# A two-layer graph attention kernel: x1 stored in the place of the head values, and two row tiles of layer 1 held back into the next entry

## The chip, the cores and the metric

The kernel runs on one core of one Trainium2 chip. The time is device microseconds from one execution of the whole program; the figure for a kernel is the median over several executions. A profile is one further look at one execution: it names engines PE (TensorE matmul; PEld is its weight load), DVE (VectorE), ACT (ScalarE), POOL (GpSimd) and SP (the engine whose queue issues the DMAs here). A "unit" below is one step of layer 0, a "row tile" 128 rows.

## The reference

Input `x` has 8 batch entries of 2048 nodes with 256 features; `adj` is one 2048 x 2048 matrix of edges for all entries.

```python
# layer 0: 8 heads of 32 features
x_proj = einsum('bnd,hdf->bhnf', x, W)
e = leaky_relu(e_src[..., :, None] + e_dst[..., None, :], 0.2)
e = e + (softplus(beta_tilde) * log(adj + 1e-6))[:, None]
attn = softmax(where(adj > 0, e, -big))
h = einsum('bhij,bhjf->bhif', attn, x_proj)          # heads side by side: 256 features
x1 = layernorm(x + h @ W_out.T)
# layer 1: one head
e = leaky_relu((x1 @ W1) @ (x1 @ W2).T, 0.2)
attn = softmax(where(adj > 0, e, -1e12))
out = layernorm(x1 + relu(attn @ (x1 @ W3)))
```

Everything is float32.

## The kernel before

Each batch entry passes through layer 0 (class `Gat`) and then layer 1 (class `Dot`). While layer 1 of entry b-1 runs, layer 0 of entry b runs between its pieces; the first entry's layer 0 runs alone, with the projections of all other entries, and the last entry's layer 1 runs alone.

**Layer 0** has 64 units per entry: four pairs of heads (`hp`) by 16 column tiles (`jt`). In a unit (`step`, L288) SP loads one row of the edge matrix (`mt`, 1 MB, two buffers), VectorE makes one 128 x 2048 tile `s` for each of the two heads (L304, four buffers), and TensorE multiplies them into `val` (the weighted sum of values, L313) and, except in the units of `SUMMED` (1, 3, 6, 8, 11, 13), into `den` (the softmax denominators, L319). The `s` of those six units are added up instead: the first by ACT (L317), the others by VectorE one unit later (L311), and one last product with ones brings the sum into `den`. After unit 15 of a pair, `finish` (L333) has ACT copy `val` to `ht` and `den` to `dn`; SP brings the denominators to a `rc` tile (L346), VectorE inverts them (L347), SP stores them to `rec_d` (L348). After each second pair SP reads them back spread over partitions, `rb` (L354), and VectorE multiplies `ht` by `rb` (L356). `ht` is two tiles, one for each two pairs, of 128 x 2048.

**`output`** (L358) goes over 16 row tiles: two products of `ht` with `wot` to `y` (L369), add of `x` (L371), layer norm (L190: statistics on VectorE, five small ACT instructions), store of x1 to `x1_d` (L373). `x` is first loaded into `h3`, a 128 x 16 x 256 tile in one buffer, by four DMAs (L365); x1 is written there too. **`turn`** (L376) transposes x1 into `x1t` (L384, L385) and replaces x1 in `h3` by x1 times W3 (L389, L391), one row tile behind.

**Layer 1** (`Dot.step`, L429) handles one row tile: transposes of its attention values `p` four at a time (L439, copied by ACT to `pts`, L441), the scores of the next row tile (L413: products `e`, leaky ReLU on ACT, mask and minimum on VectorE at L425, exponential on ACT at L426), 16 products with `h3` into `acc` (L455), and a tail with division, residual, layer norm and store. Every fourth step also makes queries `h1` (L404). `step` calls a function `fill(k)` in three places (start, after the scores, after `acc`), and the main loop puts layer 0 units there.

**Order.** TensorE's instructions stay in the order in which the code writes them (L85). Those of the other engines and of SP's queue are ordered by the framework's scheduler when the program is built; each engine then runs its own list in that order. Tiles of one tag share a ring of buffers: `ht` in the pool `chunk` has three slots of 4 KB per partition, for `dn`, `h1` and others; `mm` is a ring of three PSUM banks for `y`, transposes and scores; `whole` tiles have one buffer each, so a new tile waits until all readers of the last are done.

**Between two entries** (L491 to L507) the loop does: load of `v` for the new entry, layer 1's step 15 of the entry before, two units, `output` with a unit after rows 8 and 16, `turn` with a unit after each second row (8), the first scores, then step 0 with four units and steps 1 to 14 with 48. Layer 0 units only exist while there is a next entry (`fresh`).

Of the kernel before, what the change touches and what calls it, by code (L numbers as in the profile page):

```python
# [9 lines left out]
F32 = mybir.dt.float32  # L10
# [8 lines left out]
P = 128  # L19
# [8 lines left out]
def kernel(  # L28
# [26 lines left out]
    nc = tc.nc  # L55
    B, N, D = x.shape
    H, _, DH = w_proj.shape
    NT = N // P
    KC = D // P
    BK = 512  # L60
    NB = N // BK
    HALF = N // 2
    HP = 2
    NP = H // HP
    IG = BK // P
# [4 lines left out]
    whole = ctx.enter_context(tc.tile_pool(name="whole", bufs=1))  # L70
    wide = ctx.enter_context(tc.tile_pool(name="wide", bufs=2))
    chunk = ctx.enter_context(tc.tile_pool(name="chunk", bufs=2))
# [4 lines left out]
    def mm_tile(name):  # L77
        return ps.tile([P, BK], F32, tag="mm", name=name)

    def wide_tile(name, tag, bufs, dtype=F32):  # L80
        return wide.tile([P, N], dtype, tag=tag, name=name, bufs=bufs)
# [6 lines left out]
    ident = const.tile([P, P], F32)  # L88
# [45 lines left out]
    wot = const.tile([P, KC, D], F32)  # L134
# [8 lines left out]
    for dc in range(KC):  # L143
        t = mm_tile("w12p")
# [45 lines left out]
    def layer_norm(z):  # L190

        st = small.tile([P, nc.vector.BN_STATS_DIM], F32, name="st", bufs=2)
        nc.vector.bn_stats(st, z)
        mv = small.tile([P, nc.vector.BN_AGGR_DIM], F32, name="mv", bufs=3)
        nc.vector.bn_aggr(mv, st)  # L195
        f = small.tile([P, 4], F32, name="f", bufs=3)
        nc.scalar.activation(f[:, 0:1], mv[:, 1:2], AF.Ln, bias=eps_ln)  # L197
        nc.scalar.activation(f[:, 1:2], f[:, 0:1], AF.Exp, scale=-0.5)
        nc.scalar.mul(f[:, 2:3], mv[:, 0:1], -1.0)
        nc.scalar.activation(f[:, 3:4], f[:, 1:2], AF.Identity, scale=f[:, 2:3])  # L200
        nc.scalar.activation(z, z, AF.Identity, bias=f[:, 3:4], scale=f[:, 1:2])  # L201
# [5 lines left out]
    class Gat:  # L207


        def __init__(self, b):  # L210
            self.b = b
            self.units = ((hp, jt) for hp in range(NP) for jt in range(NT))
            self.hts = []
            self.mts = []

        def project(self):
# [10 lines left out]
            def turn(g):  # L227
# [10 lines left out]
                xts.append(xt)  # L238

            turn(0)  # L240
            for g in range(NB):
                if g + 1 < NB:
                    turn(g + 1)
                for k in range(IG):
                    it = g * IG + k
                    t = mm_tile("proj")
                    for kc in range(KC):
                        nc.tensor.matmul(t[:, 0:D + 2 * H], xts[g][:, kc, ts(k, P)], wp[:, kc, :],  # L248
                                         start=(kc == 0), stop=(kc == KC - 1))
                    nc.scalar.copy(v[:, it, :], t[:, 0:D])  # L250
                    nc.scalar.copy(ed[:, it, :], t[:, D:D + H])
                    nc.scalar.copy(es[:, :, it], t[:, D + H:D + 2 * H])
                yield
# [22 lines left out]
        def load(self):  # L276
            self.v = whole.tile([P, NT, D], F32, name="v")
            nc.sync.dma_start(self.v, v_d[self.b])
            self.re = small.tile([P, 2, NT, H], F32, name="re", bufs=2)
            nc.sync.dma_start(self.re, re_d[self.b])  # L280
# [52 lines left out]
        def finish(self, hp):  # L333


            b, lo = self.b, hp % 2 * HP * DH
            if lo == 0:
                self.hts.append(whole.tile([P, N], F32, name=f"ht{hp // 2}"))
            ht = self.hts[-1]
            for s in range(2):  # L340
                nc.scalar.copy(ht[lo:lo + HP * DH, ts(s, HALF)], self.val[ts(s, HP * DH), :])
            dn = chunk.tile([P, HALF], F32, tag="ht", name="dn", bufs=3)
            nc.scalar.copy(dn, self.den)
            rc = small.tile([P, HALF // DH], F32, name="rc", bufs=1)
            for q in range(4):
                nc.sync.dma_start(rc[ts(q, DH), :], dn[q * DH:q * DH + 1, :])  # L346
            nc.vector.reciprocal(rc, rc)  # L347
            nc.sync.dma_start(rec_d[b, hp].rearrange("q (p c) -> (q p) c", c=HALF // DH), rc)  # L348
            if lo == 0:
                return  # L350
            rb = wide_tile("rb", "d", 2)
            for a in range(2 * HP):
                src = rec_d[b, hp - 1 + a // HP, a % HP::HP, :]
                nc.sync.dma_start(rb[ts(a, DH), :].rearrange("p (s i) -> p s i", s=2),  # L354
                                  bass.AP(tensor=src.tensor, offset=src.offset, ap=[[0, DH]] + list(src.ap)))
            nc.vector.tensor_mul(ht, ht, rb)  # L356

        def output(self):  # L358


            b = self.b
            self.h3 = h3 = whole.tile([P, NT, D], F32, tag="h3", name="h3")
            xb = x[b].rearrange("(t p) d -> p t d", p=P)
            for g in range(NB):
                nc.sync.dma_start(h3[:, ts(g, IG), :], xb[:, ts(g, IG), :])  # L365
            for it in range(NT):
                y = mm_tile("y")
                for g, ht in enumerate(self.hts):
                    nc.tensor.matmul(y[:, 0:D], ht[:, ts(it, P)], wot[:, g, :], start=(g == 0), stop=(g == 1))  # L369
                z = h3[:, it, :]  # L370
                nc.vector.tensor_add(z, y[:, 0:D], z)  # L371
                layer_norm(z)
                nc.sync.dma_start(x1_d[b, ts(it, P), :], z)  # L373
                yield

        def turn(self):  # L376

            self.x1t = x1t = whole.tile([P, KC, N], F32, tag="x1t", name="x1t")
            h3 = self.h3
            for it in range(NT + 1):  # L380
                if it < NT:
                    t = mm_tile("tr1")
                    for kc in range(KC):
                        nc.tensor.transpose(t[:, ts(kc, P)], h3[:, it, ts(kc, P)], ident)  # L384
                    nc.scalar.copy(x1t[:, :, ts(it, P)], t[:, 0:D].rearrange("p (k i) -> p k i", k=KC))  # L385
                if it > 0:
                    t = mm_tile("h3p")
                    for kc in range(KC):
                        nc.tensor.matmul(t[:, 0:D], x1t[:, kc, ts(it - 1, P)], w3s[:, kc, :],  # L389
                                         start=(kc == 0), stop=(kc == KC - 1))  # L390
                    nc.scalar.copy(h3[:, it - 1, :], t[:, 0:D])  # L391
                    yield
# [90 lines left out]
    dot = None  # L483
    for b in range(1, B + 1):
        gat, fresh = gats[b - 1], gats[b] if b < B else None

        def layer_0(count):
            if fresh:
                fresh.step(count)

        if fresh:  # L491
            fresh.load()
        if dot is not None:
            dot.step()
        layer_0(2)
        for k, _ in enumerate(gat.output()):
            if k % 8 == 7:
                layer_0(1)
        for k, _ in enumerate(gat.turn()):
            if k % 2 == 1:  # L500
                layer_0(1)
        dot = Dot(gat)
        dot.step(lambda k: layer_0((2, 1, 1)[k]))
        for i in range(NT - 2):
            dot.step(lambda k: layer_0((0, 2 - (i % 2 == 1), 2 - (i % 14 == 13))[k]))
    dot.step()


# [29 lines left out]
```

## Time and profile before

| | |
|---|---|
| median of 7 executions | 4482.95 us (4480.63 to 4486.83) |
| profiled execution, its own time | 4481.61 us |
| its span, first to last instruction | 4479.8 us |
| mean granted TensorE clock | 0.983 |
| `s` on VectorE (L304) | 1024 instructions, 2345 ns each |
| sums on VectorE (L311) | 280 instructions, 2346 ns each |
| first `y` of entries 1 to 8, us from the span's start | 576.9, 1088.5, 1600.2, 2112.1, 2624.1, 3136.0, 3648.0, 4154.6 |

The middle entries are alike, some 512 us apart. In the profile's lines a group reads: start, length, engine, line, operation, tile written <- tiles read, shapes, count; in brackets the idle time of the engine before it and what ended it. Lengths of groups overlap a little, since matmuls are pipelined; the distance between the starts of two neighbours is the better measure. A line of a wait reads: who waited <- for whom, total us, times, longest us. "Granted clock" is the share of TensorE's clock that it was given.

### The profile page before, as it was taken

Reading aid. Unit: us, or ns where it says so; the run is one execution under the profiler, and the core shown is the slowest. Engines: PE = TensorE matmul, PEld = TensorE weight load, DVE = VectorE, ACT = ScalarE, POOL = GpSimd, SP = SyncE. Lnnn points to the kernel's source line nnn. Section 1 sums busy time; section 2 is a strip of 40 time slices with the busy share of each in tenths; the row PEclk is TensorE's granted clock in tenths of the full one; section 3 lists DMA queues with packets and bytes.
Section 4 is the critical chain, followed back from the end, with each engine's and each line's share of the span. In section 5 each row is a group of like instructions: output and inputs, shape, how many; then the busy total and the mean of one; then the engine's idle time right before and its main releaser. Section 6 shows DMA issues by size and latency. Waiting matters only on the chain.

```text
span 4479.8 us, 60564 instructions
## 1 busy us (share of the span) xinstructions
PE 4270.1 (95%) x24924; PEld 2222.4 (50%) x24924; DVE 3649.5 (81%) x2597; ACT 1769.9 (40%) x3739; POOL 4.5 (0%) x14
## 2 busy tenths in 40 slices
PE   6898889999999999999999999999999999999899
PEld 4443335545445544555455554555454554555566
DVE  5788798988989888888998888888988889898222
ACT  5621233334333344333433343333433343333555
POOL 0000000000000000000000000000000000000000
PEclk9999999999999999999999999999999999999999
DMA  7788865556555465555545564555545565554211
GB/s 216 255 302 322 322 211 177 190 187 214 185 184 187 167 220 174 192 187 206 197 172 183 180 220 177 192 192 192 196 173 192 180 220 185 181 181 140 69 50 40
DMA packets 252773, 852.00 MB, mean 190 GB/s; under 512 B 33616, under 2 KB 152400, under 8 KB 174928
## 3 DMA queue, kind: packets, MB, share of 16 engines
q1 hardware_dynamic: 252496, 848.13, 54.5%
q8 instruction: 195, 3.19, 0.3%
q14 instruction: 82, 0.67, 0.0%
HBM read 772.15 MB, written 75.37 MB: 189 GB/s over the span
## 4 chain that ended last, share of the span: by engine, by line
PE 66%; DVE 15%; issue 8%; ACT 4%; DMA 2%; SPq 0%; DVEq 0%; POOL 0%; POOLq 0%
PE acc L455 17%; PE e L420 15%; PE val L329 13%; DVE s L304 10%; PE den L329 9%; PE pt L439 4%; DVE d L311 3%; PE h1p L409 2%; PE proj L248 1%; DMA mt<-mt_d 1%; PE y L369 1%; ACT p L426 1%; PE h3p L389 1%; ACT h L201 1%; DVE p L425 1%
## 5 line engine op out<-in xcount | busy, mean ns | idle before, releaser
L304 DVE SCALAR_TENSOR_TENSOR s<-c,re,mt 128x2048 f32<-128x2048 f32 x1024 | 2351.1, 2345 | 194.9 <-PE den L329 122.2
L329 PE MATMUL val<-s,v 128*32 128x512 f32 x8192 | 1050.3, 605 | 91.1 <-DVE s L304 81.1
L455 PE MATMUL acc<-h,pts 128*128 128x256 f32 x4096 | 950.6, 380 | 14.4 <-ACT pts L441 13.8
L420 PE MATMUL e<-x1t,h 128*128 128x512 f32 x2048 | 903.8, 594 | 0.0
L455 PEld LDWEIGHTS acc<-h,pts 128*128 128x128 f32 x4096 | 748.2, 190 | 107.1 <-ACT pts L441 21.3
L329 PE MATMUL den<-s,re 128*32 128x512 f32 x5504 | 698.8, 596 | 0.0
L311 DVE SCALAR_TENSOR_TENSOR d<-s,re,d 128x2048 f32<-128x2048 f32 x280 | 651.5, 2346 | 0.0
L420 PEld LDWEIGHTS e<-x1t,h 128*128 128x128 f32 x2048 | 379.5, 190 | 449.9 <-issue 417.5
L329 PEld LDWEIGHTS val<-s,v 128*32 128x32 f32 x8192 | 242.7, 110 | 717.5 <-issue 522.0
L441 ACT COPY pts<-pt 128x512 f32<-128x512 f32 x512 | 296.4, 583 | 664.2 <-PE pt L439 663.9
L422 ACT ACTIVATE p<-e 128x512 f32<-128x512 f32 x512 | 303.0, 595 | 430.3 <-PE e L420 430.3
L425 DVE CUSTOM_DVE_ANT_0 p<-p,pen 128x2048 f32<-128x2048 f32 x128 | 293.0, 2289 | 202.8 <-ACT p L422 202.7
L329 PEld LDWEIGHTS den<-s,re 128*32 128x32 f32 x5504 | 192.7, 111 | 416.5 <-issue 414.7
L426 ACT ACTIVATE p<-p,neg 128x2048 f32<-128x2048 f32 x128 | 256.7, 2005 | 274.1 <-DVE neg L425 274.1
L439 PEld LDWEIGHTS pt<-ident,p 128*128 128x128 f32 x2048 | 238.0, 141 | 223.2 <-issue 166.4
L439 PE MATMUL pt<-ident,p 128*128 128x128 f32 x2048 | 318.7, 279 | 5.1 <-ACT p L426 5.1
L463 DVE TENSOR_TENSOR z<-z,x1r 128x256 f32<-128x256 f32 x128 | 54.2, 423 | 199.2 <-ACT z L462 191.1
L462 ACT ACTIVATE z<-acc,rec 128x256 f32<-128x256 f32 x128 | 60.9, 476 | 358.3 <-PE acc L455 333.5
L369 PE MATMUL y<-wot,ht 128*128 128x256 f32 x512 | 135.8, 428 | 37.7 <-DVE ht L356 36.6
L197 ACT ACTIVATE f<-mv,eps_ln 128x1 f32<-128x1 f32 x256 | 74.3, 290 | 203.4 <-DVE mv L195 202.3
L389 PE MATMUL h3p<-w3s,x1t 128*128 128x256 f32 x512 | 133.3, 386 | 12.4 <-ACT x1t L385 12.4
L369 PEld LDWEIGHTS y<-wot,ht 128*128 128x128 f32 x512 | 109.2, 217 | 70.3 <-DVE ht L356 39.4
(81 smaller groups left out, 2110.5 us busy)
## 6 DMA issues: line engine op xcount, KB each, us to landing
mt<-mt_d SPq DMA_DIRECT2D x496, 1024.0 KB, 4.9
c<-c_d SPq DMA_DIRECT2D x64, 1024.0 KB, 6.8
pen<-pen_d SPq DMA_DIRECT2D x128, 512.0 KB, 3.4
xr<-in_x_dram SPq DMA_DIRECT2D x16, 1024.0 KB, 8.2
adj_t<-in_adj_dram SPq DMA_DIRECT2D x16, 1024.0 KB, 6.8
mt_d<-mt SPq DMA_DIRECT2D x16, 1024.0 KB, 5.3
adj_r<-in_adj_dram SPq DMA_DIRECT2D x16, 1024.0 KB, 8.1
rb<-rec_d SPq DMA_DIRECT2D x64, 256.0 KB, 4.8
```

The lines of the kernel that those rows point to most:

```text
L304: nc.vector.scalar_tensor_tensor(sa, self.cs[a], self.re[:, 0, jt, h:h + 1], mt, ALU.max, ALU.mult)
L311: nc.vector.scalar_tensor_tensor(d, sa, e[:, jt - 1, h:h + 1], d, ALU.mult, ALU.add)
L329: nc.tensor.matmul(dst[ts(q, DH), ts(c, BK)], weights[q % 2], s[q % 2][:, ds(q // 2 * HALF + c * BK, BK)], start=start, stop=stop)
L369: nc.tensor.matmul(y[:, 0:D], ht[:, ts(it, P)], wot[:, g, :], start=(g == 0), stop=(g == 1))
L389: nc.tensor.matmul(t[:, 0:D], x1t[:, kc, ts(it - 1, P)], w3s[:, kc, :], start=(kc == 0), stop=(kc == KC - 1))
L420: nc.tensor.matmul(t, self.h1[:, kc, ts(it % IG, P)], self.x1t[:, kc, ts(c, BK)], start=(kc == 0), stop=(kc == KC - 1))
L422: nc.scalar.activation(p[:, ts(c, BK)], t, AF.Prelu, alpha=ALPHA)
L425: nc.vector.tensor_tensor_reduce(p, p, pen, -1.0, FMAX, ALU.add, ALU.min, neg)
L426: nc.scalar.activation(p, p, AF.Exp, bias=neg, scale=-1.0, accum_out=den)
L439: nc.tensor.transpose(t[:, ts(k, P)], p[:, ts(g * IG + k, P)], ident)
L441: nc.scalar.copy(pt, t)
L455: nc.tensor.matmul(acc, now[:, ts(k, P)], self.h3[:, j, :], start=(j == 0), stop=(j == NT - 1))
```

## The change

The two `ht` tiles become one tile of 128 x 16 x 2 x 128 (row tile, half of the features, row in the tile), with one buffer. `output` loads `x` into tiles of the `ht` ring in `chunk`, four row tiles to a load: three at the start, the fourth before row 4. x1 of a row tile is written over the head values of that row tile. `h3` is only claimed in `turn`, and `turn` transposes x1 from the heads' tile.

The main loop leaves steps 14 and 15 of layer 1 until the next entry's turn. Step 14 runs right after the load of `v`, with two units at its end; step 15 runs with 5 rows of `output` at its start, 5 rows and a unit after its first transposes, 6 rows and a unit after its products. The 48 units after `turn`'s first step are spread over 13 steps of layer 1, in the pattern 4, 4, 3. For entry 1, which has no layer 1 before it, the order is the old one. At the end of the program two steps remain instead of one.

```diff
         def finish(self, hp):
...
-            if lo == 0:
-                self.hts.append(whole.tile([P, N], F32, name=f"ht{hp // 2}"))
-            ht = self.hts[-1]
+            if hp == 0:
+                self.ht = whole.tile([P, NT, KC, P], F32, tag="heads", name="ht")
+            ht = self.ht[:, :, hp // 2, :]
             for s in range(2):
-                nc.scalar.copy(ht[lo:lo + HP * DH, ts(s, HALF)], self.val[ts(s, HP * DH), :])
+                nc.scalar.copy(ht[lo:lo + HP * DH, ts(s, NT // 2), :],
+                               self.val[ts(s, HP * DH), :].rearrange("p (t i) -> p t i", i=P))
...
-            nc.vector.tensor_mul(ht, ht, rb)
+            nc.vector.tensor_mul(ht, ht, rb.rearrange("p (t i) -> p t i", i=P))

         def output(self):
             b = self.b
-            self.h3 = h3 = whole.tile([P, NT, D], F32, tag="h3", name="h3")
             xb = x[b].rearrange("(t p) d -> p t d", p=P)
-            for g in range(NB):
-                nc.sync.dma_start(h3[:, ts(g, IG), :], xb[:, ts(g, IG), :])
+            xs = []
+
+            def load(g):
+                xs.append(chunk.tile([P, IG, D], F32, tag="ht", name="xg", bufs=3))
+                nc.sync.dma_start(xs[g], xb[:, ts(g, IG), :])
+
+            for g in range(NB - 1):
+                load(g)
             for it in range(NT):
+                if it == IG:
+                    load(NB - 1)
                 y = mm_tile("y")
-                for g, ht in enumerate(self.hts):
-                    nc.tensor.matmul(y[:, 0:D], ht[:, ts(it, P)], wot[:, g, :], start=(g == 0), stop=(g == 1))
-                z = h3[:, it, :]
-                nc.vector.tensor_add(z, y[:, 0:D], z)
+                for g in range(KC):
+                    nc.tensor.matmul(y[:, 0:D], self.ht[:, it, g, :], wot[:, g, :], start=(g == 0), stop=(g == KC - 1))
+                z = self.ht[:, it].rearrange("p g i -> p (g i)")
+                nc.vector.tensor_add(z, y[:, 0:D], xs[it // IG][:, it % IG, :])
                 layer_norm(z)
...
         def turn(self):
             self.x1t = x1t = whole.tile([P, KC, N], F32, tag="x1t", name="x1t")
-            h3 = self.h3
+            self.h3 = h3 = whole.tile([P, NT, D], F32, tag="h3", name="h3")
...
-                        nc.tensor.transpose(t[:, ts(kc, P)], h3[:, it, ts(kc, P)], ident)
+                        nc.tensor.transpose(t[:, ts(kc, P)], self.ht[:, it, kc, :], ident)
...
         if fresh:
             fresh.load()
-        if dot is not None:
-            dot.step()
-        layer_0(2)
-        for k, _ in enumerate(gat.output()):
-            if k % 8 == 7:
-                layer_0(1)
+        rows = gat.output()
+
+        def output(count):
+            for _ in range(count):
+                next(rows)
+
+        if dot is None:
+            layer_0(2)
+            for k in range(NT):
+                output(1)
+                if k % 8 == 7:
+                    layer_0(1)
+        else:
+            dot.step(lambda k: layer_0((0, 0, 2)[k]))
+            dot.step(lambda k: (output((5, 5, 6)[k]), layer_0((0, 1, 1)[k])))
...
         dot.step(lambda k: layer_0((2, 1, 1)[k]))
-        for i in range(NT - 2):
-            dot.step(lambda k: layer_0((0, 2 - (i % 2 == 1), 2 - (i % 14 == 13))[k]))
+        for i in range(NT - 3):
+            dot.step(lambda k: layer_0((0, 2 - (i % 3 == 2), 2)[k]))
+    dot.step()
     dot.step()
```

More of the change, by code (lines that the diff above doesn't have):

```diff
@@ L212, in __init__ @@
             self.units = ((hp, jt) for hp in range(NP) for jt in range(NT))
-            self.hts = []
             self.mts = []
```

## The prediction

> **What bounds the kernel now.** I read the page's first two parts, then TensorE's waits, then the stretch between two batch entries in order of time, then the busy time of each engine in pieces of that stretch.
>
> ```profile
> span 4479.8 us, 60564 instructions
> PE 4270.1 (95%) x24924; PEld 2222.4 (50%) x24924; DVE 3649.5 (81%) x2597; ACT 1769.9 (40%) x3739; POOL 4.5 (0%) x14
> PE   6898889999999999999999999999999999999899
> DVE  5788798988989888888998888888988889898222
> ```
>
> TensorE is the bound almost everywhere; VectorE (DVE) is second. What can be won without removing matmuls is TensorE's lost time only. Its waits say where that is:
>
> ```profile
> PE val L329 <- DVE s L304: 81.1, 58, 10.9
> PE y L369 <- DVE ht L356: 36.6, 7, 9.1
> PE acc L455 <- ACT pts L441: 13.8, 22, 0.8
> PE h3p L389 <- ACT x1t L385: 12.4, 14, 4.9
> ```
>
> Columns: total us, times, longest. The second line is once per entry at the first product of `output` (seven times: 9.13 in the last entry, so 4.58 in each of the other six). The order of time around one of them, TensorE alone:
>
> ```profile
> 1079.61 3.62 PE L455 MATMUL acc<-h,pts 128*128 128x256 f32 x16
> 1083.16 1.92 PE L329 MATMUL val<-s,v 128*32 128x512 f32 x16
> 1084.90 1.90 PE L329 MATMUL den<-s,re 128*32 128x512 f32 x16
> 1086.62 1.90 PE L329 MATMUL val<-s,v 128*32 128x512 f32 x16
> 1088.45 0.70 PE L369 MATMUL y<-wot,ht 128*128 128x256 f32 x2
> 1093.72 9.51 PE L369 MATMUL y<-wot,ht 128*128 128x256 f32 x30 [4.58 <-DVE ht L356]
> 1103.17 1.92 PE L329 MATMUL val<-s,v 128*32 128x512 f32 x16
> ```
>
> The last row tile of layer 1 ends, two units of layer 0 follow, then `y` stands for the normalised heads. The 30 products after the stall take 9.45 us to the next start; later 32 take 7.10 us. The window view gives the reason, and what comes next (columns: length, then busy time of PE, PEld, DVE, ACT, POOL, then the granted clock, DMA share, GB/s):
>
> ```profile
> 1073.40:1083.20 9.80, 9.18 (x56) 7.68 (x54) 3.44 (x3) 5.01 (x7) 0.00 (x0) 1.00 0.66 222
> 1083.20:1088.50 5.30, 5.30 (x50) 1.47 (x49) 2.68 (x4) 1.90 (x6) 0.00 (x0) 1.00 0.48 121
> 1088.50:1093.70 5.20, 0.65 (x5) 0.24 (x2) 5.17 (x3) 0.00 (x0) 0.00 (x0) 0.89 1.04 327
> 1093.70:1103.20 9.50, 9.47 (x34) 7.62 (x35) 6.30 (x20) 7.58 (x23) 0.00 (x0) 0.70 0.51 189
> 1103.20:1115.70 12.50, 12.50 (x82) 7.32 (x81) 12.35 (x27) 9.89 (x44) 0.00 (x0) 1.00 0.83 274
> 1115.70:1167.40 51.70, 46.98 (x308) 21.23 (x304) 51.70 (x29) 15.26 (x49) 0.00 (x0) 1.00 0.49 167
> 1167.40:1585.10 417.70, 416.31 (x2436) 209.69 (x2432) 370.19 (x237) 158.91 (x271) 0.00 (x0) 1.00 0.53 189
> ```
>
> Three things. After the stall the clock is granted at 0.70, so the stall costs 4.58 plus about 2.8 us (9.45 less 30/32 of 7.10). During step 15 of layer 1 (first row) VectorE works 3.44 of 9.80 us. In `turn` (sixth row) it works all 51.70 us: VectorE, not TensorE, sets the length there. In the last row, fifteen steps of layer 1 with 52 units of layer 0, TensorE loses only 1.4 us and VectorE is at 89%.
>
> **The change part by part.** Counts of matmuls, VectorE, ScalarE (ACT) and DMA instructions stay as they are. What moves is where they stand.
>
> *Prices.* An `s` or a denominator sum on VectorE in a dense run: 2.26 us (four `s` in 9.05). A row's add, statistics and aggregate: 0.43 + 0.43 + 0.18 = 1.03. A `val` or `den` group on TensorE: 1.74 (1083.16 to 1084.90). A step of layer 1 with no layer 0 in it, from the last entry: 4352.28 to 4367.81, 15.53. A row of `output`: 7.10 / 8 = 0.89.
>
> *Steps 14 and 15 held back.* Before, the chain from the last unit to the normalised heads (denominator out, four DMAs to `rc`, reciprocal, `rec_d`, four DMAs to `rb`, multiply) is covered by step 15 and two units, 1073.46 to 1088.4, and is 4.58 short; 4.62 of that is two `s` that VectorE took at 1086.85, ahead of the multiply. After, step 14 (15.53) and two units cover it, and the `s` of those units fit into the step before the multiply is due. I take the `y` stall as gone, and the slow clock with it. What is late next is VectorE. From the end of unit 0 to the end of `turn` it must make `s` for units 2 to 11 (20) and the sums of units 3, 6, 8 (6): 26 x 2.26 = 58.8; 16 rows, 16.5; the tails of steps 14 and 15, 2.1. Together 77.4. So from the start of step 14 to the end of `turn`: 15.53 + 3.46 (unit 0) + 77.4 + 1.85 (last `val`) = 98.2. Before, the same work took 15.53 + 93.95 (1073.46 to 1167.41) = 109.5. At most 11.3 us are saved per transition, if VectorE never rests; its rest before, in the rows, was 3.2 waiting for `y`. I take 4.0 of rest: 7.3 saved, six times, 43.8.
>
> *The last transition* has no layer 0. Before: 9.13, and the 62 products after it 15.41 against 62 x 0.222 = 13.8: some 1.6 more. There the heads were ready 19.3 us after step 15 began, but two `rb` loads were issued at 4155.30, behind an `x` load at 4154.82 that stood for step 15's last reads of `h3`. Without that wait they could go at about 4151.5, so ready after 15.5, against 15.53 of cover. Saved: between 6.9 (all of the 3.8 stays) and 10.7; I take 9.
>
> *x1 in the place of the heads.* `x` goes to three slots of the "ht" ring instead of `h3`; the four loads per entry keep their 512 KB. They wait for `dn` and the last `h1`; the latter is free after step 14's scores, its four acc groups and two units (8.2 + 5.2 us) before the first row, and a load lands in 3.9 to 8.2 us: hidden; without that cover, up to 8.2 once. The fourth load waits for row 3's add. Behind it on SP's queue stand stores of x1 and the next `mt` load, for a unit two dozen us later; `mt` lands in 4.9: hidden, else 4.9. `h3` is now claimed in `turn`; ACT's copies into it wait for step 15's last `acc`, six rows (5.3) and a `val` earlier: hidden. Next entry's first `finish` (SP's four `rc` loads and ACT's copies) waits for `turn`'s transposes, a dot step earlier: hidden. Strided heads: the multiply (2.28) and the copies (1.01) move the same elements; the nearest row for a broken-up operand is the copy to `x1t`, 0.37 for 256 elements as for the plain copy to `h3`, so I take 0.
>
> *Interleaved rows.* Rows in groups of 5, 5, 6 between pieces of step 15. The copies of `pt` (ACT, L441) now share ACT with 16 normalisations (0.29 + 0.19 + 0.20 + 0.29 + 0.60 = 1.57 each). Before shows no such mix; nearest is `turn`'s first copy to `x1t` behind the last norms: 0.80 + 0.24 per transition, and 4.91 in the last. I take the small end, within the 4.0 above; the other end is 4.9 per transition, with slow clock 7.7.
>
> The Trainium skill ("TensorE: Matmul & The Clock Gate", section "Architectural detail") has ScalarE and VectorE as strict first-in first-out queues, while TensorE may pull only weight loads ahead. This speaks against the change: a `pt` copy queued behind norms that wait for VectorE can't pass them. By the rule at its hardest the ten norms before it would hold it to the far end of the last paragraph; by the row, about 1 us.
>
> *Layer 0 packed tighter.* 48 units over 13 steps, not 14. By the last window, steps 0 to 13 would have 416.3 - 15.5 = 400.8 on TensorE and 370.2 - 2.3 - 1.0 = 366.9 on VectorE: 92%. On average there is room; locally not always. Units 11 to 14 in one step: VectorE 4 x 4.52 + 2 sums x 4.52 + 2.26 + 1.03 = 30.4, TensorE 15.53 + 6 x 1.74 = 26.0; units 4 to 7: 30.4 against 27.7. Four `s` buffers let VectorE be about one unit (4.5) ahead, which absorbs most. I take 1.5 lost per entry, seven entries, 10.5; ends 0 and 8 (4.4 + 2.7 and a little).
>
> **Sum.** 43.8 + 9 - 10.5 = 42.3. The profiled execution took 4481.6 (span 4479.8), 1.3 under the median: 4481.6 - 42.3 + 1.3 = 4440.6, so 4441.
>
> **The rivals.**
> *A, VectorE becomes the bound in the dot steps.* For it: 92%, two steps per entry over 100%, and the largest wait of TensorE is already for `s`. Against it: 89% before lost only 1.4 us in 417.7. It decides from (43.8 + 9) / 7 = 7.5 lost per entry; at 10 the sum is +17, 4500. Slower.
> *B, the wait only moves.* VectorE rests while TensorE does step 15's acc between the row groups, about as long as it rested before; then the transition gains 2 (part of the slow clock) and 12 + 6 - 10.5 = 7.5 comes out: 4475, within 0.2%. For it: `turn` stays VectorE's. Against: `s` for the next unit can start as soon as a unit two back is done.
> *C, ACT's queue or the `y` tiles' three PSUM slots stall step 15.* 4.5 of the 7.3 is lost: 6 x 2.8 + 7 - 10.5 = 13, 4470. For it: 4.91 in the last entry; against: 0.80 in the others.
>
> **How the numbers follow.** Forecast 0.58, A 0.16, B 0.09, C 0.17. About 0.2% (9 us) is what a measurement of this kernel can tell from no change: faster 0.58 + 0.17 = 0.75, same 0.09, slower 0.16. The forecast's own range is 4404 (11.3 six times, 10.7 and no loss: 78.5) to 4465. The range given reaches over C and B into A: 4404 to 4486.
>
> **What would show it.** Right: TensorE's wait of `y` for `ht` near zero; clock 1.00 through the rows; the stretch from step 14 to `turn`'s end near 102 us against 109.5; VectorE without rest from step 15 to `turn`'s end; entries about 506 apart instead of 511.9. Wrong: waits of `val` for `s` between the steps of layer 1 (A), VectorE idle for TensorE's `y` or `acc` (B), waits of `acc` for `pts` above 1 us (C), or a first `y` that stands for an `x` load.

## The result, and the profile after

The changed kernel takes 4496.62 us (median of 14 executions, 4489.8 to 4504.77) against 4483.6 for the kernel before in the same session: 1.0027 times as long, 95% interval 1.002 to 1.0034. The prediction was 4441, in a range of 4404 to 4486. It was wrong: in sign, and outside its range. The profiled execution's span is 4494.6 us, 14.8 more than before.

Part 1 of the changed kernel's page, then TensorE's waits and one of VectorE's (total us, times, longest):

```profile
span 4494.6 us, 60590 instructions
...
PE 4270.3 (95%) x24924; PEld 2218.5 (49%) x24924; DVE 3644.4 (81%) x2597; ACT 1761.3 (39%) x3739; POOL 4.5 (0%) x14
```

```profile
PE val L328 <- DVE s L303: 121.4, 62, 10.0
PE h3p L396 <- ACT x1t L392: 17.6, 8, 4.3
PE y L376 <- ACT pts L448: 9.6, 6, 1.6
PE y L376 <- DVE ht L378: 8.9, 7, 1.9
PE y L376 <- DVE ht L356: 3.6, 1, 3.6
```

```profile
DVE s L303 <- DMA mt<-mt_d: 106.2, 41, 9.0
```

The same wait of VectorE in the kernel before:

```profile
DVE s L304 <- DMA mt<-mt_d: 47.1, 26, 6.3
```

The counts of instructions on TensorE, VectorE and ACT are the same. `y` no longer waits for the heads, but for 3.6 us in the last entry, where it was 36.6 over all entries. But `val` waits 121.4 us for `s`, 81.1 before, and VectorE waits 106.2 us for `mt`, 47.1 before.

To see where, I cut each middle entry at three starts on TensorE's timeline: its first query product (`h1p`), the first product with `h3` in step 14, and the next entry's first query product. The first piece, D, holds the dot steps; the second, T, the passage between two entries. Means over the six full intervals of one profiled execution of each kernel:

| kernel | D, us | T, us | D + T |
|---|---|---|---|
| before | 403.9 | 108.1 | 511.9 |
| before, its last unit counted in D | 409.1 | 102.9 | 511.9 |
| changed | 417.2 | 96.4 | 513.6 |

The second row makes the two alike: in the old order the entry's unit 63 comes after step 14's products, in the new one before, and it costs three groups of 1.73. So the dot steps lost 8.1 us per entry and the passage won 6.5. In the dot steps of all eight entries the profile shows no wait of `val` for `s` before, and 32.1 us now; the rest of the 81.1 and 121.4 lies ahead of the first queries and in the passages. I then priced each dot step of the third entry with its own content (15.53 per step, 3.49 for queries, 1.73 per `val` or `den` group). Above that price the steps took 8.7 us in all before and 15.9 after. The difference is nearly all in one step: 7.4 above its price, where its neighbours are at 1.2 and 0.5. TensorE there, with what stands just ahead of it:

```profile
1861.23 3.64 PE L328 MATMUL val<-s,v 128*32 128x512 f32 x32
1864.69 1.90 PE L328 MATMUL den<-s,re 128*32 128x512 f32 x16
1866.52 0.66 PE L446 MATMUL pt<-ident,p 128*128 128x128 f32 x4
1867.01 7.03 PE L427 MATMUL e<-x1t,h 128*128 128x512 f32 x16
1874.50 1.05 PE L328 MATMUL val<-s,v 128*32 128x512 f32 x2 [0.46 <-DVE s L303]
1879.33 3.42 PE L328 MATMUL val<-s,v 128*32 128x512 f32 x14 [3.78 <-DVE s L303]
```

This is the stretch after the second pair of heads is finished: the first `val` and `den` above are units 1 and 2 of the third pair, and the `val` that stands is unit 3. VectorE and SP's queue in the same stretch:

```profile
1847.69 4.61 DVE L303 SCALAR_TENSOR_TENSOR s<-c,re,mt 128x2048 f32<-128x2048 f32 x2
1855.51 2.25 DVE L303 SCALAR_TENSOR_TENSOR s<-c,re,mt 128x2048 f32<-128x2048 f32 x1
1862.94 2.29 DVE L356 TENSOR_TENSOR ht<-ht,rb 128x2048 f32<-128x2048 f32 x1
1872.10 2.35 DVE L303 SCALAR_TENSOR_TENSOR s<-c,re,mt 128x2048 f32<-128x2048 f32 x1 [6.86 <-DMA mt<-mt_d]
```

```profile
1856.00 2.11 SPq L354 DMA_DIRECT2D rb<-rec_d  x3
1864.50 0.36 SPq L472 DMA_DIRECT2D out_dram<-z  x1
1864.90 1.51 SPq L422 DMA_DIRECT2D pen<-pen_d  x1
1866.46 0.91 SPq L180 DMA_DIRECT2D mt<-mt_d  x2
```

The two `s` of unit 1 end at 1852.30 and those of unit 2 at 1857.76; from then on both `mt` slots are free, for units 3 and 4, and SP issues nothing from 1858.11 on. The next in SP's list is the store of `out`, which waits for this step's layer norm until 1864.50, 6.4 us. `pen` and the two `mt` stand behind it. The `mt` of unit 3 is issued at 1866.46, 8.4 us after SP's last issue and 14.2 after its slot came free, and VectorE stands for 6.86. After TensorE's 3.78 us of idle the clock goes down; the window view of 1879.20 to 1884.00 (granted clock third from the end):

```profile
1879.20:1884.00 4.80, 4.67 (x22) 1.83 (x23) 4.80 (x4) 0.59 (x1) 0.00 (x0) 0.67 0.71 261
```

T did get shorter, but by less than was forecast; the point by point below returns to it.

### The profile page after: what moved, and what is told of

Read it like the earlier page. It is cut to its first block, busy times and chain, and to the rows that moved or that the text cites. A ratio compares the mean times of both kernels' runs of the same rounds, so it can differ in the third digit from the quotient of the medians.

```text
span 4494.6 us, 60590 instructions
## 1 busy us (share of the span) xinstructions
PE 4270.3 (95%) x24924; PEld 2218.5 (49%) x24924; DVE 3644.4 (81%) x2597; ACT 1761.3 (39%) x3739; POOL 4.5 (0%) x14
## 4 chain that ended last, share of the span: by engine, by line
PE 60%; DVE 13%; issue 7%; DMA 3%; ACT 3%; SPq 0%; DVEq 0%
PE acc L462 17%; PE e L427 15%; PE val L328 12%; DVE s L303 9%; PE den L328 8%; PE pt L446 4%; DVE d L310 3%; DMA mt<-mt_d 3%; PE h1p L416 2%; PE y L376 1%; PE h3p L396 1%; ACT ht L201 0%; ACT p L433 0%; DVE st L193 0%; ACT f L197 0%
## 5 line engine op out<-in xcount | busy, mean ns | idle before, releaser
L328 PE MATMUL val<-s,v 128*32 128x512 f32 x8192 | 1055.0, 612 | 121.6 <-DVE s L303 121.4
L376 PE MATMUL y<-wot,ht 128*128 128x256 f32 x512 | 120.7, 388 | 22.1 <-ACT pts L448 9.6
L247 PE MATMUL proj<-wp,xt 128*128 128x272 f32 x512 | 126.1, 397 | 1.5 <-ACT xt L236 0.7
```

The costliest lines, as they stand in the source:

```text
L328: nc.tensor.matmul(dst[ts(q, DH), ts(c, BK)], weights[q % 2], s[q % 2][:, ds(q // 2 * HALF + c * BK, BK)], start=start, stop=stop)
L376: nc.tensor.matmul(y[:, 0:D], self.ht[:, it, g, :], wot[:, g, :], start=(g == 0), stop=(g == KC - 1))
```

## The experiments

Theory 1: what was lost is lost to the order of SP's list in that one step, where a store that waits holds the loads behind it; the new pattern of units brought that order about when the program was built. Rival A (of the prediction; "rival 2" in some of the texts below): 48 units in 13 steps are too much for VectorE. Rival 3: the new storage costs. Rival 3b: the rows between the pieces of step 15 cost. All times below are medians, each with its ratio to the kernel before in the same session and the 95% interval.

### The storage alone

The classes of the changed kernel, with the main loop of the kernel before.

```diff
-            dot.step(lambda k: layer_0((0, 0, 2)[k]))
-            dot.step(lambda k: (output((5, 5, 6)[k]), layer_0((0, 1, 1)[k])))
+        if dot is not None:
+            dot.step()
+        layer_0(2)
+        for k, _ in enumerate(gat.output()):
+            if k % 8 == 7:
+                layer_0(1)
...
-        for i in range(NT - 3):
-            dot.step(lambda k: layer_0((0, 2 - (i % 3 == 2), 2)[k]))
+        for i in range(NT - 2):
+            dot.step(lambda k: layer_0((0, 2 - (i % 2 == 1), 2 - (i % 14 == 13))[k]))
```

> Storage alone: x1 in the place of the heads, x in three slots of the ht ring, but layer 1's steps in the old order (step 15, two units, rows with a unit after rows 8 and 16, 48 units over 14 steps). Theory 1 (what the change lost was lost to the order of SP's queue in one dot step per entry, where mt loads stand behind a store of out that waits for its layer norm): that order comes from the new pattern of units, so there is no such stall here; the y stall stays, at most 3.8 us shorter because rb no longer stands behind a load of x; 4455 to 4485, likeliest 4478. Rival 2 (VectorE is simply too full with 48 units in 13 steps): the same here, since the pattern is the old one. Rival 3 (the storage costs: strided heads, x loads through the ht ring): 4490 or more.

4484.82 us, 1.0001 (0.9992 to 1.001). D is 403.9 and T 108.1, as before, and in the third entry's dot steps SP issues its DMAs in the same order as in the kernel before. The strided heads, the copies and the new places of the `x` loads cost and gain nothing that shows. Rival 3 falls.

### The store of out from another queue

```diff
-            nc.sync.dma_start(out[self.b, ts(it, P), :], z)
+            nc.scalar.dma_start(out[self.b, ts(it, P), :], z)
```

> The changed kernel with one edit: the store of out (L472) is issued from ACT's queue instead of SP's, so that no load stands behind it. Theory 1: the wait of VectorE for mt in the dot steps (6.9 us once per entry) and with it the stall of val (about 3.7 us) and the half clock after it go; about 6 us in each of seven entries, 4450 (4440 to 4465). Rival 2: nothing changes, 4490 to 4500; the steps with four units and two sums are still there.

4457.87 us, 0.9943 (0.9928 to 0.9958). The same stretch, TensorE and SP's queue:

```profile
1854.36 0.66 PE L446 MATMUL pt<-ident,p 128*128 128x128 f32 x4
1854.86 7.03 PE L427 MATMUL e<-x1t,h 128*128 128x512 f32 x16
1861.82 1.92 PE L328 MATMUL val<-s,v 128*32 128x512 f32 x16
```

```profile
1846.12 0.42 SPq L422 DMA_DIRECT2D pen<-pen_d  x1
1846.60 0.42 SPq L180 DMA_DIRECT2D mt<-mt_d  x1
1847.16 0.80 SPq L354 DMA_DIRECT2D rb<-rec_d  x2
1848.01 9.85 SPq L180 DMA_DIRECT2D mt<-mt_d  x2
```

The `mt` loads go out without the store ahead of them, the `val` that stood now follows `e` without a gap, D falls from 417.2 to 410.8 and the step's excess from 7.4 to 0.5. T is unchanged (96.6). Seven entries by 6.4 are 45; the median is 38.8 below that of the changed kernel. Units, pattern and VectorE's work are the same, so rival A can't explain what was lost. (The order of VectorE's list changed with the edit too: at this place the multiply of the heads now comes after unit 3's `s`. In the changed kernel it stood ahead of them, but it ended at 1865.23, and VectorE then stood for the `mt` until 1872.10.) `val` now waits 0.3 us for `s` in the dot steps of all entries, where it was 32.1. VectorE still waits 88.1 us for `mt` over the whole execution, and 92.8 in the fastest kernel below: its total does not tell what is lost, the wait on TensorE does.

The control is the same edit in the kernel before:

> The same edit in the kernel before (control). Its dot steps have no wait for mt in the profile, so theory 1 expects no more than the y stall's part that SP's queue makes: 4470 to 4485. If the edit gains as much here as in the changed kernel (30 us or more), it says nothing of what the change did.

4483.62 us, 0.9999 (0.9989 to 1.0008). Where no load stood behind the store for long, the edit gives nothing.

### The store of out a step later, on SP

The store stays on SP's queue, but is written after the next step's scores and first units.

```diff
             fill(1)
+            self.store()                 # out of the step before
             acc = pacc.tile([P, D], F32, tag="acc", name="acc")
...
-            nc.sync.dma_start(out[self.b, ts(it, P), :], z)
+            self.late = it, z            # stored by self.store(); at once in the last step
```

> The changed kernel with the store of out left on SP's queue, but written one step later in the program (after the next step's scores and first units). In the built order of SP's queue the first mt load after the second pair of heads then stands ahead of that store, with its memory slot already free. Theory 1: the stall of that step goes as with ACT's queue, 4445 to 4465. If what helped in the run with ACT's queue was something else about that queue (one issue less on SP, another completion), it stays: 4490 to 4500.

4485.24 us, 1.0002 (0.9993 to 1.0011): 11 less than the changed kernel, but not the 30 or more that were expected. The dot steps did as theory 1 says: SP's queue now reads

```profile
1850.85 0.42 SPq L422 DMA_DIRECT2D pen<-pen_d  x1
1851.32 0.43 SPq L180 DMA_DIRECT2D mt<-mt_d  x1
1857.31 0.34 SPq L480 DMA_DIRECT2D out_dram<-z  x1
1857.74 0.38 SPq L180 DMA_DIRECT2D mt<-mt_d  x1
```

and the stall is gone from that step (0.5 above its price). The step behind has 3.7, and D is 412.5. But T went from 96.4 to 99.8: moving the store has also changed the order of SP's, VectorE's and ACT's lists in that passage. Moving one DMA in the program moves more than that DMA.

### Held back, but not interleaved

Steps 14 and 15 held back as in the change, all 16 rows after step 15.

```diff
-            dot.step(lambda k: (output((5, 5, 6)[k]), layer_0((0, 1, 1)[k])))
+            dot.step()
+            for k in range(NT):
+                output(1)
+                if k % 8 == 7:
+                    layer_0(1)
```

> The changed kernel without the interleaving: steps 14 and 15 are held back, but all 16 rows come after step 15, with a unit after rows 8 and 16. Theory 1: the dot steps keep their order of units, so the stall there stays if SP's queue comes out in the same order (6 us per entry); the transition loses what the mix of rows and products of step 15 overlapped (VectorE idle during acc) but not the pt copies behind norms: 4490 to 4515. Rival 3b (the interleaved rows are what costs): 4470 or less.

4483.31 us, 1.0 (0.999 to 1.0009). Below what theory 1 gave (4490), since it had counted on interleaving to help, and above what rival 3b gave. D is 417.9: in the third entry's dot steps SP's list has the same order as in the changed kernel, and the stall stays. (Whether the held-back steps or the new pattern of units brought that order about isn't shown: no run has one without the other.) T is 94.7, shorter than the 96.4 with the rows interleaved. So interleaving is a small loss here.

With `out` from ACT's queue, as above:

> Steps 14 and 15 held back, rows not interleaved with step 15, and the store of out from ACT's queue. Theory 1 in numbers: the stretch from step 14's first product with h3 to the next entry's first queries stays at 94.7 us (96.5 interleaved), the stretch of dot steps before it falls from 417.4 to about 410.7: 4483 less 7 x 6.6 = 4437 (4430 to 4448). If interleaving pays once SP's queue is free of the stores that wait: above 4455.

4424.58 us, 0.9869 (0.9851 to 0.9887), better than expected and better than both kernels. D is 410.8, and T, expected to stay at 94.7, is 92.3; why it fell was not tested. Two lines of its page:

```profile
span 4419.9 us, 60650 instructions
...
PE 4251.2 (96%) x24924; PEld 2214.1 (50%) x24924; DVE 3638.9 (82%) x2597; ACT 1751.8 (40%) x3739; POOL 4.5 (0%) x14
```

The work is the same once more; what is gone, 75 us of span against the changed kernel, was waiting.

Then with the stores of x1 from ACT's queue as well (L380 as L472):

> As the run before, with the stores of x1 (L380) from ACT's queue too. If mt loads that stand behind stores of x1 cost something in the rows, the stretch falls below 94.7 and the time by 1 to 3 us per entry: 4415 to 4435; if VectorE alone sets that stretch, no change, 4433 to 4441; ACT has 16 more issues there and may lose 1 us per entry: up to 4448.

4452.33 us, 0.9925 (0.991 to 0.994): slower than with `out` alone, outside the expectation. D is the same, T 96.1. TensorE at the start of `turn`:

```profile
1619.41 0.66 PE L391 MATMUL tr<-ident,ht 128*128 128x128 f32 x4
1626.40 2.08 PE L396 MATMUL h3p<-w3s,x1t 128*128 128x256 f32 x4 [6.33 <-ACT x1t L392]
```

ACT's copy to `x1t` comes 6.33 us late, 1.1 with x1 stored from SP; the four products after it take 2.08, where they took 1.13, and the granted clock is 0.50 from 1626.40 to 1630.60. ACT's list holds the last norms ahead of the copy, and now an issue after each norm:

```profile
1609.39 0.33 ACTq L380 DMA_DIRECT2D x_d<-ht  x1
```

With the issues ACT gets through two rows' norms in 2.93 us (the last instruction of every second row starts at 1608.78, 1611.75 and 1614.66), without them in 2.1 (1607.47, 1609.57 and 1611.66 in the run before). For 16 rows that makes some 6.7, an estimate that would cover the 5.25 by which the copy is later.

The control, both stores from ACT's queue in the kernel before:

> Control: the kernel before with both stores from ACT's queue. The y stall comes from the chain to the heads and from two s ahead of the multiply, not from SP's stores: 4470 to 4487. If it gains 20 us or more, the gain of the two runs above is not due to the held-back steps.

4489.16 us, 1.0009 (0.9999 to 1.0018), 2 above the expected range. So the queue of the stores gains nothing in the old order of steps (this run, and 4483.62 above), and the held-back steps gain nothing with `out` on SP (4483.31); the best kernel's 59.8 us need both.

### The rows' groups

Both with `out` from ACT's queue. First all rows after `acc` of step 15:

```diff
-            dot.step(lambda k: (output((5, 5, 6)[k]), layer_0((0, 1, 1)[k])))
+            dot.step(lambda k: (output((0, 0, 16)[k]), layer_0((0, 1, 1)[k])))
```

> The changed kernel with out stored from ACT's queue, and the row groups 0, 0, 16 instead of 5, 5, 6 (a unit after the scores' place and one after the 16 rows, as before). If rows between the pieces of step 15 are what costs 4.5 us per entry against the plain order (copies of pt and y sharing ACT's list and the three PSUM slots), this is within 1 us per entry of the plain order: 4420 to 4435. If the place of the units is what counts, it stays at 4450 to 4460.

4444.21 us, 0.9913 (0.9899 to 0.9928), between the two cases: T is 95.5, against 96.6 for 5, 5, 6 and 92.3 for the plain order. Rows between the pieces and the place of the units may both count; each edit also reorders the engines' lists, so their shares are not shown. Then 8, 0, 8:

> As the run before with groups 8, 0, 8: no rows directly behind the first transposes, but eight before them. If the wait of y for the copy of pt (1.6 us) alone is the cost of interleaving: about 2 us per entry better than 5, 5, 6, 4440 to 4448. If rows ahead of step 15's products cost in themselves (their norms stand in ACT's list ahead of the copies of pt): 4450 to 4462.

4488.07 us, 1.0011 (1.0002 to 1.0021), slower than either case. T is 101.5; `h3p` waits 27.5 us for ACT's copies in the whole execution, 17.7 with 5, 5, 6. (The row groups 0, 0, 16 had 26.6 and were faster, so this wait doesn't order the runs either.) `y` waits 9.2 us for the rows' adds, 22.7 with 5, 5, 6, and neither profile puts a wait of `y` down to the copy of `pt`. So less waiting at `y` did not make this order faster, and the wait for that copy is not what interleaving costs. What makes eight rows ahead of step 15 dearer than five was not tested.

### The pattern of units

```diff
-            dot.step(lambda k: layer_0((0, 2 - (i % 3 == 2), 2)[k]))
+            dot.step(lambda k: layer_0((0, 2, 2 - (i % 3 == 2))[k]))
```

In the best kernel:

> The plain order with out from ACT's queue, and the 48 units over 13 steps with the odd unit missing at the end of a step instead of after its scores (2, 2, then 2, 1). If VectorE's fullness (rival A of the prediction) had any part in the loss, moving units moves it: up to 3 us per entry either way, 4405 to 4445. By theory 1, with no waiting store in SP's queue, the same within 0.3%: 4412 to 4438.

In the changed kernel:

> The changed kernel as it is (out stored from SP's queue), with the units moved as in the run before. In the built order of SP's queue the store of out again stands ahead of two mt loads after the second pair of heads, and now unit 2 follows directly on that step's acc, with the store waiting until the norm after that acc. Theory 1: a stall there of 8 to 12 us once per entry, with a half clock after it: 4500 to 4560. Rival A: as the changed kernel, 4485 to 4505.

The first took 4484.93 us, 1.0005 (0.9995 to 1.0014): a miss by 46. The second took 4525.53, 1.01 (1.0083 to 1.0117), in its range, but not for the reason given: the stall was expected larger, 8 to 12, and its step is 6.7 above its price in the third entry (2.1 with `out` on ACT's queue), 6.7 to 9.6 over the entries, where the changed kernel had 7.2 to 9.6. The rest comes from elsewhere.

The miss by 46 teaches something, since the text of the passage between entries is the same as in the best kernel. There D grew by 3.5 and T by 5.8. VectorE in T, the best kernel first, then with the units moved, and there TensorE too:

```profile
1583.94 6.88 DVE L303 SCALAR_TENSOR_TENSOR s<-c,re,mt 128x2048 f32<-128x2048 f32 x3 [4.45 <-DMA mt<-mt_d]
1593.05 0.42 DVE L470 TENSOR_TENSOR z<-z,x1r 128x256 f32<-128x256 f32 x1 [2.23 <-ACT z L469]
```

```profile
1604.97 2.35 DVE L303 SCALAR_TENSOR_TENSOR s<-c,re,mt 128x2048 f32<-128x2048 f32 x1 [3.33 <-DMA mt<-mt_d]
1612.85 0.42 DVE L470 TENSOR_TENSOR z<-z,x1r 128x256 f32<-128x256 f32 x1 [5.52 <-ACT z L469]
...
1619.78 2.34 DVE L303 SCALAR_TENSOR_TENSOR s<-c,re,mt 128x2048 f32<-128x2048 f32 x1
```

```profile
1622.17 1.49 PE L328 MATMUL val<-s,v 128*32 128x512 f32 x11 [1.99 <-DVE s L303]
```

In the first, three `s` are made ahead of the tail of step 15. In the second only one is; the other head's `s` of the same unit stands in VectorE's list behind the tail, for which VectorE idles 5.52 us, and behind rows of `output`. It ends at 1622.12, and `val` waits 1.99 us for it after row 8, where it did not wait in the best kernel. Its `mt` was there at 1604.97, for the first head's, so here it was no load that held it. Moving units in the dot steps had reordered VectorE's list in a passage that was not touched. This is not the stall of the changed kernel, which came from SP's list; that it is all of the 5.8, and what the 3.5 in D are, was not shown.

## Why the prediction was wrong, point by point

**The y stall.** Right. `y` waited 36.6 us for the heads, and waits 3.6 now, all in the last entry, where I had 0 to 3.8 and took about 2. The low clock behind it in the rows is gone too.

**The six full transitions.** Predicted 7.3 each; measured 6.5 (102.9 to 96.4). About right, in part by luck: two errors inside partly cancel. From the end of unit 0 to the first queries my sum was 77.4 + 1.85 and 4.0 of rest, 83.3. The third passage in the window view:

```profile
1601.00:1685.90 84.90, 77.02 (x485) 43.12 (x477) 75.73 (x80) 34.81 (x127) 0.00 (x0) 0.98 0.56 195
```

84.9, with VectorE at work for 75.7 and at rest for 9.2, most of it in two places (the first wait begins 1.9 us ahead of the stretch):

```profile
1603.94 0.42 DVE L378 TENSOR_TENSOR ht<-y,xg 128x256 f32<-128x256 f32 x1 [4.84 <-PE y L376]
1646.55 4.61 DVE L303 SCALAR_TENSOR_TENSOR s<-c,re,mt 128x2048 f32<-128x2048 f32 x2 [5.38 <-PE den L328]
```

The first is the sign that I had named for rival B. In the plain order, with `out` stored from ACT's queue, the same stretch is

```profile
1581.20:1663.60 82.40, 78.76 (x485) 43.17 (x477) 76.66 (x80) 33.51 (x125) 0.00 (x0) 0.98 0.59 204
```

82.4, with 5.7 of rest. I expected the interleaved rows to fill VectorE's rest; it is longer with them.

**Interleaved rows.** I took the small end, and nothing beyond the 4.0 of rest. `y` waited 1.6 us in each of the six passages for the copy of `pt`, and the first `h3p` of `turn` 2.0 to 2.1 for the copy to `x1t` (0.80 + 0.24 before). In five of the six the clock then went down at the start of `turn`; one of them:

```profile
2149.30:2155.90 6.60, 4.55 (x22) 3.25 (x22) 4.76 (x4) 5.08 (x22) 0.00 (x0) 0.74 0.36 102
```

In the plain order with `out` from ACT's queue that `h3p` waits 1.1, and the clock goes down in one passage of six, later in `turn`. That the later 5.38 us of VectorE's rest follows from this was not tested.

**The last transition.** Predicted 9 saved. From step 14's first product with `h3` to the first queries it took 72.7 before, 67.5 without unit 63, and 61.0 after: 6.5. That is near the 6.9 that I gave for the case that all of the 3.8 stays, and 3.6 did stay.

**Layer 0 packed tighter.** This is the step that failed. I took 1.5 lost per entry with ends 0 and 8, from VectorE's fullness. Measured were 8.1, and with it came about the total of rival A (4500 against 4496.62). But the reason was another. With the store of `out` on ACT's queue the same units lose 410.8 - 409.1 = 1.7: for the tighter packing itself the 1.5 was about right, though that all of it is VectorE's fullness is not shown. Of the two steps that I had marked as over 100% for VectorE, the one with units 4 to 7 (30.4 against 27.7) stands 0.5 above its price, as most steps do in the kernel before; the one with units 11 to 14 stands 1.2 above, of which 0.54 is `den` waiting for ACT's copy `dn`. The step that lost 7.4 has one unit fewer. What I had not priced was that another pattern of units makes another list for SP. I had followed the loads that the change moves past, and found them hidden, but not the store of `out`, which the change does not name. The trace of before had the sign, in SP's queue after the second pair of heads:

```profile
1848.14 0.42 SPq L180 DMA_DIRECT2D mt<-mt_d  x1
1849.23 0.79 SPq L354 DMA_DIRECT2D rb<-rec_d  x2
1853.74 0.36 SPq L465 DMA_DIRECT2D out_dram<-z  x1
```

There an `mt` load goes out between the `rb` loads and ahead of the same store, which then waits until 1853.74. That order was not fixed by the code. (VectorE's 47.1 us of waiting for `mt` were no sign: 39.1 of them lie ahead of the first queries of the first entry.)

**Storage and queues.** The `x` loads, the strided heads, the later claim on `h3`: priced at 0, and the run with the storage alone gives 1.0001. What remains open is 3.6 us before the first queries of entry 1 (655.6 to 659.3), of which 3.1 also show there, in a profiled span 3.8 longer than that of before, while the median is the same. In the other runs these queries start between 655.7 and 661.5.

**Sum by steps.** Dot steps of six entries at 8.17 and of one at 6.9 lost, six transitions at 6.45 and the last at 6.5 saved, entry 1 at 3.6 lost: 55.9 - 45.2 + 3.6 = 14.3, of 14.8 between the spans. Without the store in SP's queue the change gives -26.5, without interleaving too -59.8: the forecast of -42 lies between what this form of the idea could give and what a coarser form gave.

## What to carry to other kernels

Where a scheduler orders a DMA queue when the program is built, a change in the order of compute work is also a change of that list, and of the other engines' lists: look in the trace for stores that stand in it waiting for a result, and for what is behind them, before counting engine time. Here a store of 128 KB kept SP's list standing for 6.4 us in the entry shown, and moving it off that list gained 39 us in all; issuing it from the engine that makes its data removed the stall. And try coarse orders before fine mixtures: with the same store moved, rows after step 15 were 33 us faster here than rows mixed into it.

## What the runs showed of the hardware that I had not expected

An idle stretch of TensorE of 3.78 us, with two products before it and 0.46 of idle before those, was enough for a granted clock of 0.67 over the 4.8 us after it. Shorter waits did not always leave the clock alone. In the changed kernel the same wait of 2.0 to 2.1 us at the start of `turn` was followed by a clock of 0.50 for some 3.3 us in five passages (2667.50 to 2670.80 is one) and by none in the sixth (1.00 from 1119 to 1140). In `turn` of the kernel before, waits of 0.83 and 1.22 us close together left the clock at 1.00; in the best kernel the same two waits went with 0.50 from 1654.60 to 1657.90 in one passage.

Sixteen more stores per passage issued from ACT went along with a copy by ACT that came 6.33 us late, where one was 1.1 late without them, though ACT itself makes what is stored. Each issue took 0.33 us of ACT's queue, and two rows' norms 2.93 us where they took 2.1.
